# Attention and mixture-of-experts block: three quarters of the tokens' routed experts by sorted group slots instead of all experts for all tokens

## The chip, the core and the metric

One NeuronCore of a Trainium2 chip runs the whole block in one launch. The metric is device time in microseconds (us) of one execution. TensorE does matrix products (PE in the profile, PEld its weight loads), VectorE is DVE, ScalarE is ACT, GpSimd is POOL. SyncE (SP) computes nothing here; it issues transfers (DMAs). Each engine runs its own instructions strictly in order, so an instruction that waits holds up all that stand behind it on that engine.

## The reference, cut to what matters

Two sequences of 1024 tokens of width 128. First causal attention (8 heads, 2 key/value heads through a latent width of 32), with a layernorm before and after and a residual. Then the routed block, here the part that the change touches:

```
scores = sigmoid(x @ gate_weight.T)                    # 32 experts, in 4 groups of 8
sc = scores + gate_bias
group_scores = top_k(sc.reshape(T, 4, 8), 2)[0].sum(-1)
_, gidx = top_k(group_scores, 2)                       # each token keeps 2 of the 4 groups
masked = where(expert in a kept group, sc, -inf)
_, topidx = top_k(masked, 6)                           # 6 experts, all in the kept groups
tw = scores[topidx] / sum * 0.2
routed = sum over the 6: tw * (silu(x @ w_gate[e]) * (x @ w_up[e])) @ w_down[e]
shared = (silu(x @ shared_w_gate) * (x @ shared_w_up)) @ shared_w_down
lg = topidx[:, 0] // 2                                 # one of 16 anchors
anchor = 0.1 * (silu(x @ anchor_w_gate[lg]) * (x @ anchor_w_up[lg])) @ anchor_w_down[lg]
x = x + layernorm(routed + shared + anchor)
```

Expert width is 64, anchor width 32, all numbers are 32-bit floats. The anchor follows from the best expert, so it lies in that expert's group: a token needs only the experts and anchors of its two groups.

## The kernel before, in words

A batch entry is `b` (0 or 1), a tile is 128 tokens, a block is 512 tokens (`BC`), so there are 16 tiles and four blocks.

**Attention** (`attention`, L535 on) goes through 40 steps: a step is one piece of 512 keys for one unit (batch, key/value head, 256 queries). Its order of work is written by hand. Step by step PE gets scores (`numerators`, L464 and L478), the maxima of later units (`maxima`, L399, reduced by DVE at L416), and the weighted values and sums of the step before (L501, L510). Batch 0 goes through its query blocks from first to last, batch 1 from last to first. A block of queries on the diagonal has its exponentials masked by POOL (L487).

**Side work** is a list `side` of generators. Each call of `tick()` advances the generator at the head of the list by one piece and emits its instructions at that place of every engine's order. Attention ticks about twice a step. `route(b)` is such a generator. For all 8 tiles of a batch entry it makes the attention's output projection (L621), the two layernorms, the transposed input `hT` (L313), the logits (L668), then on DVE the choice of groups and experts (`max`, `match_replace`, L692 to L748), and at last the table of weights `cw`: 48 numbers a token (32 experts, 16 anchors). It is transposed and written to DRAM as `cw_rows[b]` (L756).

**Experts** (`experts`, L762 on) does every expert for every token. The 32 experts make 16 chunks of two, the 16 anchors 4 chunks of four; a chunk is 128 hidden units wide. All gate and up weights lie in SBUF (`wg_sb`, `wu_sb`), the down weights too (`wd_sb`). For one block of 512 tokens and each of the 20 chunks (`hidden`, then `down` two chunks later):

- SP issues the spread of the weights from `cw_rows`: rows of DRAM, each broadcast to the 64 or 32 partitions of its expert (L770), into one of 8 buffers;
- PE multiplies `pg` (L775) and `pu` (L776), 512 columns each;
- ACT takes silu (L779), DVE multiplies by `pu` (L780) and by the spread (L781);
- PE adds the chunk to `oacc` with the hidden tile as the moving operand of 512 columns (L785).

The shared expert is one more, first in a block (L791 to L800). `rest()` transposes the 512 results, takes the last layernorm, adds the residual on POOL (L826) and writes them out (L827). The calls stand in the order attention, then blocks (0,0), (0,1), (1,0), (1,1); `route(0)` runs inside attention, `route(1)` inside the first two blocks. PSUM has 7 banks in rotation (`bank`) and one for accumulation (`acc`). PE, DVE, ACT and POOL run in the order in which the program is written; SP's order is left to the scheduler.

Of the kernel before, what the change touches and what calls it, by code (L numbers as in the profile page):

```python
# [17 lines left out]
P = 128  # L18
# [7 lines left out]
def attn_moe_block(  # L26
# [33 lines left out]

    nc = tc.nc
# [20 lines left out]
    NCE = E // EC  # L82
    NCA = A // AC
    NCH = NCE + NCA

# [39 lines left out]
    wg_sb = const.tile([P, NCH, P], F32, name="wg_sb")  # L125
    wu_sb = const.tile([P, NCH, P], F32, name="wu_sb")
    wd_sb = const.tile([P, NCH, D], F32, name="wd_sb")
    for dst, ew, aw in ((wg_sb, w_gate, anchor_w_gate), (wu_sb, w_up, anchor_w_up)):
        nc.sync.dma_start(
            out=dst[:, 0:NCE, :].rearrange("h c (e i) -> h (c e) i", i=MI),  # L130
            in_=ew.rearrange("e h i -> h e i"),
        )
        nc.sync.dma_start(
            out=dst[:, NCE:NCH, :].rearrange("h c (a i) -> h (c a) i", i=AI),
            in_=aw.rearrange("a h i -> h a i"),
        )
    nc.sync.dma_start(
        out=wd_sb[:, 0:NCE, :], in_=w_down.rearrange("(c e) i h -> (e i) c h", e=EC)
    )
    nc.sync.dma_start(  # L140
        out=wd_sb[:, NCE:NCH, :],
        in_=anchor_w_down.rearrange("(c a) i h -> (a i) c h", a=AC),
    )
    swg_sb = const.tile([P, SI], F32, name="swg_sb")
    nc.sync.dma_start(out=swg_sb, in_=shared_w_gate)
    swu_sb = const.tile([P, SI], F32, name="swu_sb")
    nc.sync.dma_start(out=swu_sb, in_=shared_w_up)
    swd_sb = const.tile([SI, D], F32, name="swd_sb")
    nc.sync.dma_start(out=swd_sb, in_=shared_w_down)
# [33 lines left out]
    dram = ctx.enter_context(tc.tile_pool(name="dram", bufs=1, space=bass.MemoryType.DRAM))  # L183
    cw_rows = [dram.tile([E + A, T], F32, name=f"cw_rows{b}") for b in range(B)]
# [3 lines left out]
    ctx.enter_context(tc.manual_schedule(engines={E_.PE, E_.DVE, E_.Activation, E_.Pool}))  # L188
# [136 lines left out]
    def project(b, c):  # L325
# [44 lines left out]
        (b, g, q) for b in range(B) for q in (range(NQ) if b == 0 else reversed(range(NQ)))  # L370
# [164 lines left out]
    def attention(done_with):  # L535
# [39 lines left out]
        for k, (u, s) in enumerate(steps):  # L575
# [11 lines left out]
            tick()  # L587

# [3 lines left out]
            if waiting:  # L592
                last = waiting[0]
                sums(*waiting, o[last])
                if last[0] != u[0]:
                    done_with(last[0])
            waiting = (u, s, pr)
            tick()
            if any(need[j] - done > j - k - 1 for j in range(k + 1, len(steps))):
                one_item()  # L600
                tick()
        weigh(waiting)
        sums(*waiting, o[waiting[0]])
        done_with(waiting[0][0])


    routed = {}

    def route(b):

        while any(u not in ot for u in units if u[0] == b):
            yield
        x1 = x_sb[b]
        norm = Norm(NT, f"attn{b}")
        halves = [range(c * 4, c * 4 + 4) for c in range(NT // 4)]
        an = [work.tile([P, 4, D], F32, tag="xn", name=f"an{b}{c}", bufs=4) for c in range(NT // 4)]
        for c, tiles in enumerate(halves):
            po = bank(f"po{b}{c}")
            for i, t in enumerate(tiles):
                for g in range(G):  # L620
                    nc.tensor.matmul(  # L621
                        po[:, ts(i, P)], lhsT=ot[b, g, t // TQ][:, ts(t % TQ, P)], rhs=ao[:, g, :],
                        start=(g == 0), stop=(g == G - 1),
                    )
            nc.scalar.copy(an[c].rearrange("p t d -> p (t d)"), po)
            yield
        for c, tiles in enumerate(halves):
            norm.stats([an[c][:, i, :] for i in range(4)], 4 * c)
            yield
# [7 lines left out]
        for c, tiles in enumerate(halves):  # L637
# [6 lines left out]
        norm = Norm(NT, f"moe{b}")  # L644
        for c, tiles in enumerate(halves):
# [9 lines left out]
        hT = const.tile([P, T], F32, name=f"hT{b}")  # L655
        hs = []
        for c, tiles in enumerate(halves):
            h = work.tile([P, 4, D], F32, tag="xn", name=f"h{b}{c}", bufs=4)
            for i, t in enumerate(tiles):
                norm.apply_act(h[:, i, :], x1[:, t, :], t)  # L660
            hs.append(h)
            yield
        for c, h in enumerate(hs):
            transposed(h, hT[:, ts(c, BC)], f"h{b}{c}")
            yield
        pl = bank(f"pl{b}")
        for t in range(NT):
            nc.tensor.matmul(pl[:, ts(t, E)], lhsT=hT[:, ts(t, P)], rhs=gwT, start=True, stop=True)  # L668
        score = small.tile([P, NT, E], F32, tag="score", name=f"score{b}", bufs=1)
        loaded[0] = None  # L670
        nc.scalar.activation(score.rearrange("p t e -> p (t e)"), pl[:, 0 : NT * E], AF.Sigmoid)
        yield
        sc = small.tile([P, NT, E], F32, tag="sc", name=f"sc{b}", bufs=1)
        nc.vector.tensor_tensor(
            sc, score, bias_sb.unsqueeze(1).to_broadcast([P, NT, E]), ALU.add
        )
# [3 lines left out]
        g8 = small.tile([P, NT, NG, 8], F32, tag="g8", name=f"g8_{b}", bufs=1)  # L680
        gs = small.tile([P, NT, 16], F32, tag="gs", name=f"gs{b}", bufs=1)
        nc.gpsimd.memset(gs[:, :, NG:8], -BIG)
        nc.gpsimd.memset(gs[:, :, 8:16], BIG)
        ms = small.tile([P, NT, E + 8], F32, tag="ms", name=f"ms{b}", bufs=1)
        nc.gpsimd.memset(ms[:, :, E : E + 8], BIG)
        first = small.tile([P, NT, 8], F32, tag="first", name=f"first{b}", bufs=1)
        nc.gpsimd.memset(first, BIG)

        cw = work.tile([P, NT, E + A], F32, tag="cw", name=f"cw{b}", bufs=1)
        for t in range(NT):  # L690
# [5 lines left out]
        gtop = small.tile([P, NT, 8], F32, tag="gtop", name=f"gtop{b}", bufs=1)  # L696
        for t in range(NT):
            nc.vector.max(gtop[:, t, :], gs[:, t, 0:8])
        nc.vector.memset(gtop[:, :, TOPG:8], BIG)
        yield  # L700
        grep = small.tile([P, NT, 16], F32, tag="grep", name=f"grep{b}", bufs=1)
        for t in range(NT):
            nc.vector.match_replace(grep[:, t, :], gtop[:, t, :], gs[:, t, :], BIG)
        yield

        gm = small.tile([P, NT, NG], F32, tag="gm", name=f"gm{b}", bufs=1)
        nc.vector.tensor_tensor(gm, grep[:, :, 0:NG], gs[:, :, 0:NG], ALU.not_equal)
        nc.vector.tensor_scalar(gm, gm, -0.5, 2.0 * HALF, ALU.add, ALU.mult)
# [3 lines left out]
            gm.unsqueeze(3).to_broadcast([P, NT, NG, EG]),  # L712
# [3 lines left out]
        etop = small.tile([P, NT, 8], F32, tag="etop", name=f"etop{b}", bufs=1)  # L716
        for t in range(NT):
# [3 lines left out]
        yield  # L721
        erep = small.tile([P, NT, E + 8], F32, tag="erep", name=f"erep{b}", bufs=1)
        frep = small.tile([P, NT, E + 8], F32, tag="frep", name=f"frep{b}", bufs=1)
        for t in range(NT):
            nc.vector.match_replace(erep[:, t, :], etop[:, t, :], ms[:, t, :], BIG)
        yield
        for t in range(NT):
            nc.vector.match_replace(frep[:, t, :], first[:, t, :], ms[:, t, :], BIG)
        yield
# [4 lines left out]
        tot = small.tile([P, NT], F32, tag="tot", name=f"tot{b}", bufs=1)  # L734
        nc.vector.tensor_reduce(tot, em, AX.X, ALU.add)
        nc.vector.tensor_scalar(tot, tot, 1e-20, None, ALU.add)
        nc.vector.reciprocal(tot, tot)
        nc.vector.tensor_scalar(tot, tot, 0.2, None, ALU.mult)
# [150 lines left out]
```

## Time and profile before

| what | value |
|---|---|
| device time, median of 3 runs | 480.56 us (479.4 to 482.61) |
| the profiled execution | 480.45 us |
| its span, first to last instruction | 478.7 us |
| TensorE clock granted, mean | 0.984 |
| PE, DVE, ACT, POOL busy | 95%, 63%, 46%, 7% of the span |
| attention ends, first block begins | 233 us |
| block (0,0), (0,1), (1,0), (1,1) from | 233.4, 298.5, 357.4, 412.8 us |
| moved over DMA | 29.26 MB |

The profile of one execution lists for each engine its busy time, then groups of equal instructions by line of the kernel, with count, summed time, mean time of one, and the idle time that stood in front of them with its releaser. The chain that ended last is followed back from the last instruction and says which work set the end. A 32-bit matrix product appears as two MATMUL records, each with its own weight load, so 80 products give 160 records. Matmul records overlap: the distance between their starts, not their duration, is what one costs.

### The profile page before, as it was taken

To read this page: it belongs to the slowest core of one execution; us is meant where nothing else is said; L and a number is where in the kernel's file an instruction comes from. 1 tells how busy PE (TensorE), PEld (TensorE's weight loads), DVE (VectorE), ACT (ScalarE), POOL (GpSimd) and SP (SyncE) were. 2 spreads that over 40 slices of the span, in tenths; PEclk is the share of its full clock that TensorE was granted. 3 is DMA by queue.
4 is the path that set the end of the run, shared out by engine and by line. 5 is a ranking of instruction groups with operands and counts; after the bars stand their busy time and mean duration, and the time that the engine had idled before them with its cause. 6 is when DMAs were issued, how large, how long until landed. Compare 5 with 4: busy or idle time off the path is not lost.

```text
span 478.7 us, 8959 instructions
## 1 busy us (share of the span) xinstructions
PE 453.1 (95%) x3427; PEld 223.7 (47%) x3427; DVE 303.3 (63%) x943; ACT 219.6 (46%) x427; POOL 33.5 (7%) x55
## 2 busy tenths in 40 slices
PE   8997999999999999988869999999999999999991
PEld 5554554544555555555345444544434444344440
DVE  4468766466756887797335575489656755466552
ACT  3454556554554747746642646432225422252222
POOL 2000000000000201002100110000001100001001
PEclk9999999999999999999979999999999999999996
DMA  7820000000000000000521333223151353124100
GB/s 218 222 86 1 2 1 2 1 1 3 1 1 3 2 1 3 1 2 19 176 68 55 100 109 96 66 83 109 51 163 60 118 134 109 66 91 136 58 1 22
DMA packets 27355, 29.26 MB, mean 61 GB/s; under 512 B 8272, under 2 KB 16112, under 8 KB 27312
## 3 DMA queue, kind: packets, MB, share of 16 engines
q1 hardware_dynamic: 26976, 28.15, 19.5%
q8 instruction: 27, 0.44, 0.4%
q10 hardware_dynamic: 336, 0.54, 0.3%
q14 instruction: 16, 0.13, 0.1%
HBM read 27.23 MB, written 1.44 MB: 60 GB/s over the span
## 4 chain that ended last, share of the span: by engine, by line
PE 70%; DVE 16%; issue 10%; ACT 1%; DMA 1%; POOL 0%; POOLq 0%; ACTq 0%; DVEq 0%
PE pg L775 12%; PE pu L776 12%; PE oacc L785 11%; DVE nm L416 8%; PE sm L399 7%; PE s L464 5%; PE o L501 4%; PE o L510 4%; PE pp L352 3%; PE po L621 2%; DVE parts L432 2%; PE psh L791 2%; DVE nm L434 1%; PE s L478 1%; PE sm L409 1%
## 5 line engine op out<-in xcount | busy, mean ns | idle before, releaser
L416 DVE TENSOR_REDUCE nm<-sm 128x1 f32<-128x512 f32 (+2 forms) x192 | 92.7, 548 | 53.1 <-PE sm L409 37.0
L780 DVE TENSOR_TENSOR hid<-hid,pu 128x512 f32<-128x512 f32 x80 | 54.8, 686 | 75.9 <-PE pu L776 56.8
L484 ACT ACTIVATE pr<-s 128x512 f32<-128x512 f32 (+1 forms) x160 | 75.5, 558 | 55.5 <-PE s L478 55.5
L779 ACT ACTIVATE hid<-pg 128x512 f32<-128x512 f32 x80 | 47.8, 597 | 115.5 <-PE pg L775 103.5
L775 PE MATMUL pg<-hT,wg_sb 128*128 128x512 f32 x160 | 83.4, 603 | 0.0
L776 PE MATMUL pu<-hT,wu_sb 128*128 128x512 f32 x160 | 82.1, 594 | 0.0
L785 PE MATMUL oacc<-hid,wd_sb 128*128 128x512 f32 x160 | 80.9, 595 | 0.0
L781 DVE TENSOR_TENSOR hid<-hid,spread 128x512 f32<-128x512 f32 x80 | 58.0, 725 | 2.7
L776 PEld LDWEIGHTS pu<-hT,wu_sb 128*128 128x128 f32 x160 | 30.7, 192 | 38.8 <-issue 37.9
L785 PEld LDWEIGHTS oacc<-hid,wd_sb 128*128 128x128 f32 x160 | 30.1, 190 | 39.3 <-issue 31.5
L464 PE MATMUL s<-qT,kT 32*128 32x256 f32 (+1 forms) x640 | 46.9, 381 | 1.0 <-DVE nm L416 1.0
L775 PEld LDWEIGHTS pg<-hT,wg_sb 128*128 128x128 f32 x160 | 29.3, 192 | 35.7 <-issue 34.8
L399 PE MATMUL sm<-kT,qT 32*128 32x512 f32 (+3 forms) x384 | 44.3, 525 | 0.8 <-DVE nm L416 0.3
L501 PE MATMUL o<-pr,v 128*32 128x256 f32 (+1 forms) x640 | 39.4, 364 | 2.1 <-POOL pr L487 1.9
L464 PEld LDWEIGHTS s<-qT,kT 32*128 32x128 f32 x640 | 32.0, 184 | 16.2 <-issue 10.1
L510 PE MATMUL o<-pr,ones 128*32 128x256 f32 (+1 forms) x640 | 39.3, 363 | 0.0
L487 POOL TENSOR_SCALAR_AFFINE_SELECT pr<-pr 128x1024 f32<-128x1024 f32 x16 | 17.8, 1112 | 196.3 <-ACT pr L484 196.3
L501 PEld LDWEIGHTS o<-pr,v 128*32 128x32 f32 x640 | 16.7, 109 | 23.2 <-issue 10.1
L510 PEld LDWEIGHTS o<-pr,ones 128*32 128x32 f32 x640 | 17.0, 109 | 20.5 <-issue 11.6
L399 PEld LDWEIGHTS sm<-kT,qT 32*128 32x128 f32 x384 | 16.8, 183 | 11.9 <-issue 4.2
L826 POOL TENSOR_TENSOR y<-y,x 128x512 f32<-128x512 f32 x4 | 5.1, 1267 | 192.3 <-DVE y L295 150.7
L478 PE MATMUL s<-mT,ones 32*128 32x512 bf16 (+1 forms) x160 | 16.9, 353 | 1.5 <-DVE mT L447 1.5
(163 smaller groups left out, 365.1 us busy)
## 6 DMA issues: line engine op xcount, KB each, us to landing
spread<-cw_rows SPq DMA_DIRECT2D x128, 128.0 KB, 2.9
spread<-cw_rows SPq DMA_DIRECT2D x64, 64.0 KB, 2.0
out_dram<-y SPq DMA_DIRECT2D x4, 256.0 KB, 2.3
x<-in_L_attn_x_dram SPq DMA_DIRECT2D x2, 256.0 KB, 4.1
wq_sb<-in_L_attn_wq_dram ACTq DMA_DIRECT2D x2, 256.0 KB, 4.2
wo_sb<-in_L_attn_wo_dram SPq DMA_DIRECT2D x1, 512.0 KB, 6.5
x<-in_L_attn_x_dram SPq DMA_DIRECT2D x1, 512.0 KB, 7.6
cw_rows<-cwT SPq DMA_DIRECT2D x4, 96.0 KB, 1.9
```

What stands on the lines that cost most here:

```text
L399: nc.tensor.matmul(banks[r][:, at : at + k1 - k0], lhsT=qT[ts(r, L), g, ts(qt, P)], rhs=kT[ts(r, L), g, k0:k1], start=(at == 0), stop=Fals ...
L416: nc.vector.tensor_reduce(nm[:, k0 // BC, j, r : r + 1], banks[r][:, at : at + k1 - k0], AX.X, ALU.max, negate=True,)
L464: nc.tensor.matmul(banks[r][:, at : at + n], lhsT=kT[rows, g, ts(kt, P)], rhs=qT[rows, g, q * QC + lo : q * QC + lo + n], start=(i == 0), ...
L484: nc.scalar.activation(pr[:, r, 0:m], banks[r][:, 0:m], AF.Exp)
L501: nc.tensor.matmul(o[ts(r, L), lo : lo + n], lhsT=qkv[b][2][:, kt, ts(g, L)], rhs=pr[:, r, at : at + n], start=(kt == 0), stop=False, skip ...
L510: nc.tensor.matmul(o[ts(r, L), QC + lo : QC + lo + n], lhsT=ones32, rhs=pr[:, r, at : at + n], start=False, stop=True, skip_group_check=True,)
L775: nc.tensor.matmul(pg, lhsT=wg_sb[:, c, :], rhs=hT[:, cols], start=True, stop=True)
L776: nc.tensor.matmul(pu, lhsT=wu_sb[:, c, :], rhs=hT[:, cols], start=True, stop=True)
L779: nc.scalar.activation(hid, pg, AF.Silu)
L780: nc.vector.tensor_tensor(hid, hid, pu, ALU.mult)
L781: nc.vector.tensor_tensor(hid, hid, spread, ALU.mult)
L785: nc.tensor.matmul(oacc, lhsT=wd_sb[:, c, :], rhs=hid, start=False, stop=(c == NCH - 1))
```

## The change

Tokens are split. `sparse` is batch 0 and the first half of batch 1 (12 tiles, 1536 tokens); `dense` is the second half of batch 1 (4 tiles, one block). The dense block keeps the 20 chunks of 512 columns, in another order (by group: 4 expert chunks and 1 anchor chunk, five times 128 hidden units a group), with gate and up weights fetched by group. The sparse tokens go another way:

1. At the start the gate and up weights are copied from DRAM to a DRAM tensor `wgu` ordered by group; only the down weights are kept in SBUF. A DRAM tensor `placed` of 15 x 256 rows of 176 numbers is filled with zeros.
2. `route(b, t0, n)` works on parts: (0, tiles 0 to 7), (1, tiles 0 to 3), (1, tiles 4 to 7). For sparse parts it keeps, per token, a row of 128 inputs and 48 weights, and which two groups were chosen.
3. `place()` counts: with triangular and all-ones products on PE, each token's rank in each of its two groups; each group gets whole slots of 256 places (at most 15 slots for 3072 rows). DVE works out each row's place and each slot's group number. POOL then issues 24 indirect DMAs (12 tiles x 2 groups) that scatter 128 rows of 704 bytes each into `placed`, with a small memset ahead of each.
4. `Slots.begin()` loads the group numbers into registers of PE and SP, fetches the rows of the first two slots and transposes them.
5. `Slots.run()` goes through 15 slots: 5 chunks in pairs, gate and up products of 256 columns, silu, two multiplications, and down products with the hidden tile as the stationary operand (128 tokens) and 128 columns of `wd_sb`, picked by the slot's group number. Ahead of that SP fetches the slot's weights (655 KB, by group number), the spread of its weights (six DMAs) and its rows; ACT writes the transposed weights to DRAM and the slot's results to `results`.
6. `gathered(i)`, three times for four tiles each, is side work of the dense block: POOL issues 8 indirect DMAs that gather each token's two result rows, DVE adds both and the shared expert's, and the last layernorm follows.

Attention now goes through batch 1 from first to last query block, with two ticks in batch 1 where there was one. SP's order becomes that of the program too. The list of side work is: the projections, `route(0,0,8)`, `route(1,0,4)`, `place()`, `begin()`, `route(1,4,4)`, and after the slots the three `gathered`.

```diff
+    SL = 256
+    sparse, dense = [(0, 0, NT), (1, 0, NT // 2)], [(1, NT // 2, NT // 2)]
+    NS = TOPG * NTS * P // SL + NG - 1
...
-        (b, g, q) for b in range(B) for q in (range(NQ) if b == 0 else reversed(range(NQ)))
+        (b, g, q) for b in range(B) for q in range(NQ)
...
+        for i, (b, _, t) in enumerate(tiles_of):
+            for k in range(TOPG):
...
+                nc.gpsimd.memset(between, 0.0)
+                move = nc.gpsimd.indirect_dma_start(
+                    out=placed[:, :],
+                    out_offset=bass.IndirectOffsetOnAxis(ap=place_of[:, k, i : i + 1], axis=0),
+                    in_=rows[b][:, t, :], in_offset=None,
+                )
+                tc.declare_no_dep(move.ins, group="placed", reason="no two places are the same")
+                tc.add_to_no_dep_group("placed", move.ins)
+            if i % 2:
+                yield
...
+        def begin(self):
...
+            _, self.numbers = nc.values_load_multi_w_load_instructions(
+                group_no[0:1, 0:16], engines=(E_.PE, E_.SP), min_val=0, max_val=NG - 1,
...
+            self.fetch_rows(0)
+            self.fetch_weights(0)
+            self.fetch_rows(1)
+            yield
+            yield
+            self.turn_rows(0)
+            yield
+            self.fetch_spread(0)
+            self.turn_rows(1)
+            routed["slots"] = True
+            yield
...
+        def turn_rows(self, i):
...
+            pt = bank(f"pt_s{i}")
+            for j in range(JL):
+                nc.tensor.transpose(pt[:, ts(j, P)], self.got[i][:, j, 0:D], ident)
+            for j in range(JL):
+                nc.tensor.transpose(
+                    pt[0 : E + A, SL + j * P : SL + (j + 1) * P], self.got[i][:, j, D : D + E + A], ident
+                )
+            cwT = quarter(f"cwTs{i}")[0 : E + A, :]
+            nc.scalar.copy(cwT, pt[0 : E + A, SL : 2 * SL])
+            nc.scalar.dma_start(out=cw_slots[i], in_=cwT)
+            self.hTp[i] = quarter(f"hTp{i}")
+            nc.scalar.copy(self.hTp[i], pt[:, 0:SL])
...
+        def fetch_spread(self, i):
...
+            own = cw_slots[i][bass.ds(self.numbers[i] * GW, GW), :]
+            half = own[0:EG, :].rearrange("(c e) t -> e c t", e=EC)
+            for e in range(EC):
+                nc.sync.dma_start(
+                    out=t[ts(e, MI), 0:EH, :], in_=half[e].partition_broadcast(MI)
+                )
+            for a in range(AC):
+                nc.sync.dma_start(
+                    out=t[ts(a, AI), EH, :], in_=own[EG + a, :].partition_broadcast(AI)
+                )
...
+        def run(self):
+            while "slots" not in routed:
+                tick()
+            ahead = []
+            for i in range(NS):
+                for k in range(-(-NC // 2)):
+                    ahead.append((i, k, self.hidden(i, k)))
+                    if len(ahead) > 2:
+                        self.down(*ahead.pop(0))
+                    if k == 0:
+                        self.fetch_weights(i + 1)
+                        self.fetch_spread(i + 1)
+                        self.fetch_rows(i + 2)
+                    if k == 1:
+                        self.turn_rows(i + 2)
+                    tick()
...
+    def gathered(i):
...
+        y = [work.tile([P, TB, D], F32, tag="y", name=f"y{name}{k}") for k in range(TOPG)]
+        for t in range(TB):
+            for k in range(TOPG):
+                nc.gpsimd.indirect_dma_start(
+                    out=y[k][:, t, :], out_offset=None, in_=results[:, :],
+                    in_offset=bass.IndirectOffsetOnAxis(
+                        ap=place_of[:, k, i + t : i + t + 1], axis=0
+                    ),
+                )
+        sh = shared(name, slice(t0 * P, (t0 + TB) * P), b)
+        yield
+        py = bank(f"py{name}")
...
+        yield
+        flat = [t.rearrange("p t d -> p (t d)") for t in y]
+        nc.vector.tensor_tensor(flat[0], flat[0], py, ALU.add)
+        nc.vector.tensor_tensor(flat[0], flat[0], flat[1], ALU.add)
+        yield
+        yield from normed(name, b, t0, y[0])
...
+    some = Slots()
+    side += [*(route(*part) for part in sparse), place(), some.begin()]
+    side += [route(*part) for part in dense]
+    attention()
+    some.run()
+    for b, t0, n in dense:
+        while (b, t0) not in routed:
             tick()
+        for c in range(t0 // TB, (t0 + n) // TB):
+            experts(b, c)
```

In the dense block, `tick()` is called twice a chunk. The weights of a slot lie in one of two buffers, the spreads in one of three, the rows in one of three, and the two gathered tiles `y` (two tiles a `gathered`) in the two buffers of that kind.

## The prediction

> **What bounds the kernel now.** I read the page's busy shares first, then the chain, then the costliest groups, and from there the expert stage alone.
>
> ```profile
> PE 453.1 (95%) x3427; PEld 223.7 (47%) x3427; DVE 303.3 (63%) x943; ACT 219.6 (46%) x427; POOL 33.5 (7%) x55
> PE 70%; DVE 16%; issue 10%; ACT 1%; DMA 1%; POOL 0%; POOLq 0%; ACTq 0%; DVEq 0%
> L775 PE MATMUL pg<-hT,wg_sb 128*128 128x512 f32 x160 | 83.4, 603 | 0.0
> L785 PE MATMUL oacc<-hid,wd_sb 128*128 128x512 f32 x160 | 80.9, 595 | 0.0
> L781 DVE TENSOR_TENSOR hid<-hid,spread 128x512 f32<-128x512 f32 x80 | 58.0, 725 | 2.7
> ```
>
> PE is the bound. In the expert stage no DMA is waited for. The chain there, piece by piece (start, length, what):
>
> ```profile
> 140.88 1.98 PE po L621 x16
> 192.10 1.76 PE pl L668 x16
> 357.38 1.86 PE psh L791 x4
> 382.59 0.86 PE pg L775 x2
> 385.16 0.86 PE pg L775 x2
> 412.75 1.86 PE psh L791 x4
> ```
>
> A product of 512 columns costs 0.86 us of PE, a chunk (three) 2.57 us (382.59 to 385.16), an undisturbed block 55.4 us (357.4 to 412.8). The first two rows price small products: 8 of 128 columns take 1.98 us, 0.25 each; 8 of only 32 columns still take 1.76, 0.22 each, so below 128 columns it isn't the columns that set the price (PEld is busy 1.86 of the 1.92 us around those eight: the weight load does).
>
> Transfers: how long SP is held by a spread's issue, and when it lands (the answer for L770 at 226 to 236 us, then for L756); and a POOL instruction over 128 rows.
>
> ```profile
> L770 SPq DMA_DIRECT2D spread<-cw_rows x15: 495/595/1184, 226.0 to 235.5; - x15
> DMA to landing us min/median/max: 2.8/3.1/3.7
> L756 SPq DMA_DIRECT2D cw_rows<-cwT x4: 302/308/325, 224.1 to 345.4; - x4
> DMA to landing us min/median/max: 1.9/1.9/3.2
> L487 POOL TENSOR_SCALAR_AFFINE_SELECT pr<-pr 128x1024 f32<-128x1024 f32 x16 | 17.8, 1112 | 196.3 <-ACT pr L484 196.3
> ```
>
> Last, what an idle PE costs afterwards (stretches; the number after POOL's is the granted clock):
>
> ```profile
> 243.00:245.00 2.00, 0.00 (x0) 0.00 (x0) 0.98 (x2) 0.94 (x2) 0.00 (x0) 1.00 0.38 125
> 247.00:249.00 2.00, 2.00 (x11) 2.00 (x11) 0.00 (x0) 0.00 (x0) 0.00 (x0) 0.50 0.36 119
> ```
>
> About 4 us of idleness were followed by some 7 us at half clock: 3.4 us lost.
>
> **What is removed.** Three of four blocks: 233.4 to 298.5, 298.5 to 357.4, 357.4 to 412.8, so 179.4 us. The fourth, with the tail, is 66.0 us (412.8 to 478.7) and stays.
>
> **Attention, +6.** The half route of batch 1 moves in from the first blocks: 8 output products 1.98, 4 transposes 0.66, 4 logit products 0.96: 3.6 us of PE. `place()` adds 13 narrow bf16 products at about 0.1 (L409: four in 0.40): 1.3. DVE gets some 14 us of routing (half of the 16 tiles' rows of statistics, maxima and replacements) and about 4 us for `place()`; DVE is busy 65.9 of 88 us in batch 1, so between 0 and 18 us of it shows; I take 3, since PE is at 82 of 88. The end gains: three short diagonal steps that wait for POOL's mask become one, -2. Attention would end at 239 us, if nothing in it waited.
>
> **The scatter, +32.** Counting the pieces of side work against the ticks: the 24 scatters are emitted from step 36 (of 0 to 39), and `turn_rows(0)`, which needs all of them landed, stands in PE's order just ahead of step 38. The cover is two steps. Maxima are finished by then, and such a step takes 3.0 us (scores 1.08, products against ones 0.25, values 0.85, sums 0.85). The last step to the first product after it took 5.9 us in the profile (227.4 to 233.3), so step 38 begins at 239 - 5.9 - 3.0 = 230 and step 36 at 224. POOL: 24 x (indirect DMA + memset 0.12). The trace has no indirect DMA. Below, 0.30, the shortest issue on SP; above, 2.4, if each waited for a landing. I take 1.1, what POOL itself needs for an instruction over 128 rows (L487), because it is POOL that has to issue these, each with a list of 128 places. 24 x 1.22 = 29.3: 224.5 to 253.8. Landing 1.9: 255.7. `fetch_rows(0)` on SP, which stands behind that wait with the weights of slot 0 behind it: 2.3 to land (as the 256 KB output does): 258. PE stands still for 28 us, with ACT, DVE and steps 38 and 39 behind it. With transposes 0.7 and the half clock 3.4: 32. The slots begin at 271. Loading the group numbers into PE's registers falls into the same wait; it costs nothing unless that wait is gone, then at most some us.
>
> The Trainium skill, "DMA: Bandwidth & Descriptors", section "Anatomy of one DMA", gives a DMA issued from GpSimd about 2.0 us plus its bytes at 436 GB/s, most of it completion; no run here shows that yet. By the page, 90 KB take 2.2 us each, and if scatters did not overlap their sum would be 53 us and not 29; the nearest row here, 1.9 us for SP's 96 KB, is a landing and not an issue.
>
> **The slots, +136.** PE per slot: 10 products of 256 columns at 0.43 (half of 0.86; not below 0.25) 4.3; 10 of 128 columns at 0.24, 2.4; four transposes about 0.5: 7.2 us. DVE 2 x 1.4 + 0.8 = 3.6, ACT about 3.5: hidden. But there is a ring: turning slot i+1's rows lets ACT write its weights; SP's spread of i+1 waits for that write; the rows of slot i+2 stand behind that spread on SP; and PE turns them in its own order, four chunks later. Its length: transposes 0.7, ACT copy 0.45, issue and landing 1.9 plus 0.1; six spread issues (2 x 0.6, 4 x 0.4) 2.8 and their register arithmetic 0.6 (0 to 2, not in the trace); rows to landing 2.3 to 2.8: about 9.2 us. It is longer than 7.2, so it sets the pace: 12 turns x 9.2 = 110, the first 3.7, the last two slots and the rest 18. `route(1,4,4)` runs there and costs ACT its table loads (1.28 us each): +4. Sum 136. Data: 1.5 MB a slot, 160 GB/s at this pace; the trace held 240 to 260 in most of the first 28 us, so bandwidth is no bound unless small rows halve it.
>
> **The gathers, +31.** The dense block keeps 55.4. In it, DVE's add of `gathered(0)` stands behind chunk 1, about 7 us in. The results land 2.9 us after the last product, 8 gathers x 1.1 = 8.8, landing 2: 13.7 us in. PE runs on as long as banks last (7): it loses about 4.5. The next `gathered` needs both `y` buffers: free only when the output has landed, 7.5 us after the statistics begin (470.2 to 477.7 in the tail shown by the trace), plus one chunk of DVE 1.4, gathers 8.8, landing 2, adds 1.4: 21 to 21.5 us from add to add. In that time DVE's order lets PE have three chunks, 7.7. So 13.8 lost, twice. With 4.5 that is 32, less 0.9 for the merged shared product. Everything of it hangs on DVE's order; the spreads queued behind the output DMA on SP are two buffers ahead.
>
> **Start and others, 0.** The reordering copies and the zero fill queue on SP behind the inputs, in the first 40 us, and are wanted after 220. The outer time is 480.45 - 478.7 = 1.75; the profiled run is 0.1 below the median.
>
> **Sum:** 478.7 - 179.4 + 6 + 32 + 136 + 31 = 504.3; with 1.75: 506 us.
>
> **Rivals.**
> - *The indirect DMAs are cheap* (ends faster). For it: the issue time needn't grow with the pieces; SP issued the 1024 pieces of `wo` in 0.39 us and the 64 rows of a spread in 0.60. Each 0.1 us less is worth 2.4 in the scatter and about 2.2 in the gathers. At 0.30: 506 - 0.8 x 46 = 469. It decides from 0.53 us down, where the time equals that of before. Against: the issue is not SP's.
> - *The ring fits into PE's 7.2 us*: 12 x 2.0 less, 482. For it: landings here go down to 1.8. Against: seven issues stand in a row in it.
> - *Transfers crowd*: rows of 1 KB, and a write of weights that shares the engines with 655 KB. At 11.5 us a slot 12 x 2.3 more, 534.
> - *Indirect DMAs follow one another with their landings*: 2.4 us each, 1.2 us more for 48, most of it exposed, 560. Against: scatters are declared independent.
>
> **How the numbers follow.** Mine 0.48 (490 to 522), cheap 0.18, ring hidden 0.14, crowding 0.12, serial 0.08. Predicted: 506. The range 466 to 536 leaves out the serial case, the low end of the cheap one and the high end of crowding. Less than 1% (4.8 us) can't be told from no change. Faster: cheap 0.16, ring 0.05, mine 0.01: 0.22. Same: 0.02 + 0.06 + 0.03 = 0.11. Slower: 0.44 + 0.03 + 0.12 + 0.08 = 0.67.
>
> **What would show it.** PE idle for some 28 us ahead of the first turned rows, released by a DMA, with POOL busy all that time and the clock at half after it; slots 9 us apart with PE waiting for rows; two stops of DVE of over 10 us in the dense block, released by gathers. The prediction is wrong if POOL's issues are under 0.6 us, if turned rows never wait, or if gathers land before their adds.

## The result, and the profile after

The changed kernel takes 543.4 us (median of 4 runs, 540.9 to 547.0) where the kernel before took 480.7 beside it (4 runs, 479.4 to 482.6): 1.131 times the time, 95% interval 1.123 to 1.138. Forecast were 506, with 466 to 536. The direction came out, and so did the stop at the scatter and the ring of the slots; the move was 62.7 us, where the forecast, from the 480.6 known then, was 25.4. The profiled run took 543.64 us and spans 541.9.

First the page's header, busy shares, slices of the span and chain, of the kernel after:

```profile
span 541.9 us, 10069 instructions
PE 429.9 (79%) x3726; PEld 266.8 (49%) x3726; DVE 285.3 (53%) x969; ACT 221.6 (41%) x455; POOL 84.1 (16%) x155
...
PE   8989999999989888973047687888678886649991
...
POOL 3000000000121002008820010000000014535000
PEclk9999999999999898777559897998989998587997
...
PE 36%; DVE 19%; DMA 15%; POOL 9%; issue 8%; ACT 5%; SPq 5%; POOLq 0%; DVEq 0%; ACTq 0%
```

TensorE was 95% busy and 70% of the chain; now it is 79% and 36%. It lost only 23 us of work (453.1 to 429.9) for three blocks removed, since the 15 slots bring theirs back in smaller products. DMA and POOL, once 1% of the chain together, hold 24%. In the slices PE falls to 3 and 0 while POOL shows 8 and 8: that is the scatter. The 6s and the 4 near the end, again beside POOL, are the gathers. The granted clock is low there, and already in the end of attention, ahead of the scatter (the first two 7s). TensorE was at half clock for 108 us of the trace, against 17 before.

The stop before the slots, on PE's timeline (start, length, engine, line, what, and in brackets the idle time before it and what ended it):

```profile
247.43 1.07 PE L547 MATMUL o<-pr,ones 128*32 128x256 f32 x16 [0.37 <-issue]
278.64 0.69 PE L961 MATMUL pt_s<-ident,got 128*128 128x128 f32 x2 [30.15 <-DMA got<-placed]
...
289.35 0.83 PE L547 MATMUL o<-pr,ones 128*32 128x256 f32 x16
290.11 1.13 PE L1000 MATMUL pgs<-hTp,wbs 128*128 128x256 f32 x4
```

Forecast were 28 us; it is 30.15. Attention's last steps (until 290.2) come behind the stop. POOL in the same stretch, its first three scatters:

```profile
244.34 1.17 POOL L898 DMA_INDIRECT placed<-rows,place_of  x1 [2.81 <-DVE place_of L892]
245.52 0.11 POOL L897 MEMSET between<- 128x1 f32 x1
245.81 0.96 POOL L898 DMA_INDIRECT placed<-rows,place_of  x1 [0.18 <-issue]
246.78 0.11 POOL L897 MEMSET between<- 128x1 f32 x1
247.08 1.03 POOL L898 DMA_INDIRECT placed<-rows,place_of  x1 [0.19 <-issue]
```

An indirect DMA holds POOL for 0.96 us, and with memset and gaps the 24 follow each other at 1.28 (244.3 to 273.7); I had put 1.22. But the first starts at 244.3 and not at 224.5.

What waited, in total, times, longest (answer on waits, kernel after):

```profile
PE pt_s L961 <- DMA got<-placed: 57.4, 14, 30.1
...
PE pyg L1099 <- DVE shg L1063: 18.0, 3, 9.7
...
DVE yg L1105 <- DMA yg<-results,place_of: 14.4, 3, 5.8
...
PE rank L844 <- DVE mb L837: 3.9, 1, 3.9
...
POOL yg L1089 <- DMA out_dram<-yg: 3.8, 2, 2.0
```

The first line is the ring: beside the 30.1 of the scatter, PE waited 27 us for rows at 13 other slots, which went by every 10.2 us (turned rows at 320.3 and, ten slots later, at 422.4). The second is where TensorE itself stops beside the gathers: the shared expert's product for a gathered group waits for VectorE's multiplication, which in the two long ones stands in VectorE's order behind the add and norm of the group before. The third is VectorE's wait for the gathers. The fourth belongs to `place()`, inside attention. The last is the wait that I had blamed for the stops at the gathers, and it is small.

| stretch | forecast | measured | off by |
|---|---|---|---|
| first scatter | 224.5 | 244.3 | +19.8 |
| first product of a slot | 271 | 290.1 | +19.1 |
| slots | 136 | 149.0 (to 439.1) | +13.0 |
| dense block, gathers, tail | 97.3 | 102.8 (to 541.9) | +5.5 |

The last three add up to the 37.6 by which the span was missed.

### The profile page after: what moved, and what is told of

Read it like the earlier page. It is cut to its first block, busy times and chain, and to the rows that moved or that the text cites. A ratio compares the mean times of both kernels' runs of the same rounds, so it can differ in the third digit from the quotient of the medians.

```text
span 541.9 us, 10069 instructions
## 1 busy us (share of the span) xinstructions
PE 429.9 (79%) x3726; PEld 266.8 (49%) x3726; DVE 285.3 (53%) x969; ACT 221.6 (41%) x455; POOL 84.1 (16%) x155
## 4 chain that ended last, share of the span: by engine, by line
PE 36%; DVE 19%; DMA 15%; POOL 9%; issue 8%; ACT 5%; SPq 5%; POOLq 0%; DVEq 0%; ACTq 0%
DVE nm L453 7%; DMA got<-placed 7%; PE sm L436 5%; PE s L501 4%; POOL placed L898 4%; POOL yg L1089 4%; PE o L538 4%; PE o L547 3%; SPq L983 3%; DMA wbs<-wgu 3%; PE pp L389 2%; PE pa L1000 2%; SPq L979 2%; DMA cw_slot<-cwTs 2%; PE oacc L1159 2%
## 5 line engine op out<-in xcount | busy, mean ns | idle before, releaser
L1008 DVE TENSOR_TENSOR hids<-hids,pus 128x512 f32<-128x512 f32 x30 | 20.6, 686 | 71.0 <-ACT hids L1007 47.4
L501 PE MATMUL s<-qT,kT 32*128 32x256 f32 (+1 forms) x640 | 53.3, 402 | 5.8 <-DVE nm L453 5.2
L961 PE MATMUL pt_s<-ident,got 128*128 128x128 f32 x30 | 7.5, 338 | 57.4 <-DMA got<-placed 57.4
L1089 POOL DMA_INDIRECT yg<-results,place_of x24 | 24.3, 1011 | 129.8 <-issue 125.7
L1023 PEld LDWEIGHTS ys<-wd_sb,hids 128*128 128x128 f32 x300 | 41.7, 197 | 2.7
L1023 PE MATMUL ys<-wd_sb,hids 128*128 x300 | 41.4, 279 | 0.0
L1007 ACT ACTIVATE hids<-pgs 128x512 f32<-128x512 f32 x30 | 17.9, 596 | 37.5 <-PE pgs L1000 37.4
L1000 PE MATMUL pgs<-hTp,wbs 128*128 128x256 f32 x120 | 31.8, 389 | 0.0
L1000 PE MATMUL pus<-hTp,wbs 128*128 128x256 f32 x120 | 30.8, 379 | 0.0
L1149 ACT ACTIVATE hid<-pg 128x512 f32<-128x512 f32 x20 | 11.8, 597 | 44.5 <-PE pg L1145 44.5
```

The lines of the kernel that those rows point to most:

```text
L501: nc.tensor.matmul(banks[r][:, at : at + n], lhsT=kT[rows, g, ts(kt, P)], rhs=qT[rows, g, q * QC + lo : q * QC + lo + n], start=(i == 0), ...
L1000: nc.tensor.matmul(p[:, lo : lo + SL], lhsT=wb[:, m, ts(c, P)], rhs=hT, start=(lo == 0), stop=(c == pair[-1]), skip_group_check=True,)
L1007: nc.scalar.activation(hid[:, 0:n], pg[:, 0:n], AF.Silu)
L1008: nc.vector.tensor_tensor(hid[:, 0:n], hid[:, 0:n], up, ALU.mult)
L1023: nc.tensor.matmul(o[:, ts(j, D)], lhsT=hid[:, at : at + P], rhs=w, start=(c == 0 and j == 0), stop=(c == NC - 1), skip_group_check=True,)
L1089: nc.gpsimd.indirect_dma_start(out=y[k][:, t, :], out_offset=None, in_=results[:, :], in_offset=bass.IndirectOffsetOnAxis(ap=place_of[:, k ...
```

## The experiments

Each is one profiled run against the kernel before on the same chip (477.8 to 480.9), unless an interval is given. The kernel after varied by 6 us from run to run, so single runs are read by their stages, and differences of 3 us are not read at all.

### Where attention's 24 us come from

**a1_ascending and a5_ascending_timed**: the kernel before with one edit.

```diff
-for q in (range(NQ) if b == 0 else reversed(range(NQ)))
+for q in range(NQ)
```

> The kernel before with one edit: attention goes through batch 1 from first to last query block. Theory (attention got long because routing and counting fill VectorE in batch 1): the order alone costs little, the first expert block begins at 230 to 237 us (233.4 before), total 478 to 486. Rival (the order itself, with the long steps last): the first block begins at 243 us or later, total 490 or more.

> The kernel before with the second batch of the attention taken from first to last, as in the earlier run of the same edit (471.8 us), now with an interval: 470 to 474, about 1.5% under the kernel before. If that run was a lucky one: 476 to 482.

471.8, then 472.99 (4 runs), ratio 0.985, interval 0.982 to 0.988. The first expert block begins at 231.4 (before: 233.3), as expected:

```profile
231.40 1.07 PE L791 MATMUL psh<-hT,swg_sb 128*64 128x512 f32 x2
```

The rest of the gain, which I had not expected, comes behind it, so the total fell below the forecast 478. The kernel before, then this one, by stretches (PE, PEld, DVE, ACT, POOL busy, then granted clock and DMA):

```profile
243.00:250.00 7.00, 3.42 (x15) 3.42 (x16) 2.47 (x5) 0.96 (x3) 0.00 (x0) 0.67 0.25 76
```

```profile
243.00:250.00 7.00, 7.00 (x27) 3.86 (x26) 3.88 (x13) 1.78 (x3) 0.00 (x0) 1.00 0.21 76
```

The stop in the first block, with its half clock, is gone. So the order is no cost: alone it gains 1.5%, and this one-line edit is the fastest kernel of the study. Why the stop goes with the order was not tested, and the kernel after has no expert block at that place, so nothing shows that it keeps this part of the gain.

**a2_ascending_two_ticks**: the same, and two ticks for one in batch 1 (`if u[0]: tick()` twice a step).

> The kernel before with the ascending order and two ticks in batch 1, so that routing of batch 0 is packed into the first half of batch 1's steps, as in the changed kernel; routing of batch 1 stays under the expert blocks. Theory: packing costs up to 6 us (first block at 234 to 241), and the rest of the 18 to 20 us is the half route of batch 1 and the counting. Rival (the packing is all of it): first block at 250 us or later.

482.8; the first block begins at 242.4:

```profile
242.38 1.07 PE L795 MATMUL psh<-hT,swg_sb 128*64 128x512 f32 x2
```

Packing the side work costs 11.0 us, not up to 6. Part of it is the clock: from 185 to 220 it was granted at 0.85 here, 5 us of full clock lost, and at 1.00 in a1.

**a4_one_tick**: the kernel after without the doubled ticks (the two `if u[0]: tick()` removed).

> The kernel after without the doubled ticks of the attention's second batch. The question is which of two terms makes up the 24 us by which the scatters of the kernel after came later than the first expert block of the kernel before. Theory (the route of the second batch's first half and the places are one chain of small VectorE instructions; the scatters can start only at its end, packed or not): the attention ends about 11 us earlier, and the chain that is then left runs with TensorE stopped; the scatters begin at 240 to 248 as in the kernel after (244.3), and the time is within 5 us of 543. Rival (the packing itself costs the 11 us that it cost in the kernel before): the scatters begin at 231 to 237 and the time is 530 to 536.

553.5, and both theories missed: the scatters begin at 259.9, later than in the kernel after. Its PE timeline:

```profile
234.65 0.83 PE L547 MATMUL o<-pr,ones 128*32 128x256 f32 x16
242.54 1.63 PE L350 MATMUL pt_h<-ident,rows 128*128 128x128 f32 x4 [7.05 <-ACT rows L342]
244.85 1.92 PE L715 MATMUL pl<-upT,hT 128*128 128x32 f32 x8 [0.68 <-ACT hT L351]
256.21 0.22 PE L840 MATMUL rank<-mb,before 128*128 128x48 bf16 x1 [9.45 <-DVE mb L833]
```

Attention is over at 235.5, 4 us behind a1. Then route and places run alone, a chain of short instructions with PE stopped for most of the time, and the first scatter starts 24 us later. So doubled ticks lose 11 us inside attention to save more behind it.

**a6_begin_behind**: the slots' beginning, with the first turned rows, moved behind attention's last step.

```diff
-side += [*(route(*part) for part in sparse), place(), some.begin()]
-side += [route(*part) for part in dense]
+side += [*(route(*part) for part in sparse), place()]
 attention()
+side += [some.begin(), *(route(*part) for part in dense)]
```

> The kernel after, with the beginning of the slots (rows 0 and 1, weights, the first turned rows) written behind the attention's last step instead of among its side work. In the kernel after, TensorE's stop of 30.15 us stands ahead of the last steps of the attention, which end at 290.2. Theory (these steps depend on nothing that is scattered and run while POOL scatters): they end at about 258, the turned rows still come at about 279, the slots begin 8 to 10 us earlier: 533 to 536. Rival (the scatters come later by as much, or the route of the last four tiles takes the gain): within 3 us of 543.

538.6, half of the forecast gain, and not more than the kernel after varies from run to run. By stages, the slots begin at 281.3 for 290.1, the 8 to 10 us forecast, but end only 2.4 us earlier (436.7 for 439.1). All steps but the last ran on (their last product starts at 252.2), and then PE stopped again, for another reason. The waits of this kernel between 240 and 290 us:

```profile
PE o L538 <- POOL pr L524: 21.4, 1, 21.4
PE pt_s L961 <- DMA got<-placed: 2.4, 1, 2.4
```

The last step's causal mask is a POOL instruction, and it stood behind the 24 scatters. One wait took the place of the other. Why the slots then lost most of their lead was not tested.

### What the stop at the scatter is

**s1_half_scatter**: the kernel after, `for k in range(1)` for `range(TOPG)` at the scatters.

> The kernel after, with only the first choice of each token scattered: 12 of the 24 scatters and of their memsets. The other choice's places stay zero, so its rows are left out of the computation; the number of slots, their loads and matmuls stay as they are. Theory (the stop of TensorE before the first turned rows is the POOL's own string of scatters, 1.265 us from one to the next in the kernel after): 12 x 1.265 = 15.2 us less, the wait of pt_s falls from 30.15 to about 15, the span by 15 to 18 (half clock after a shorter stop included), time 525 to 529. Rival (the stop is the landing of the writes, or something else that is late, such as the route of the last four tiles): the wait stays above 25 us and the time above 537.

526.1, and the longest wait for the turned rows is halved (waits of this kernel, 230 to 300 us):

```profile
PE pt_s L961 <- DMA got<-placed: 18.3, 3, 15.0
```

30.1 to 15.0 for 12 scatters less: 1.26 each. The stop is POOL's string of issues. The last scatter starts at 273.7 and the rows that wait for it are issued at 276.2, so only 2.5 us are end and landing. The Trainium skill, "DMA: Bandwidth & Descriptors", section "Anatomy of one DMA", calls descriptor generation small and most of its 2.0 us completion. Here landings overlapped, and what added up was POOL's 0.96 us of issue with the memset and the gaps; the measurement decides.

### What the rows of the ring stand behind

Five kernels change only SP's work of a slot. The original order is: weights of slot i+1 (640 KB), its spread (two transfers of 256 KB, four of 32), rows of slot i+2 (176 KB).

**r1_rows_first**: rows ahead of both. **r5_rows_second**: rows between them.

```diff
+self.fetch_rows(i + 2)        # r1
 self.fetch_weights(i + 1)
+self.fetch_rows(i + 2)        # r5
 self.fetch_spread(i + 1)
-self.fetch_rows(i + 2)
```

> The changed kernel with the rows of slot i+2 issued on SP ahead of weights and spread of slot i+1. Theory (a ring through ACT's write, the spread and the rows sets the slots' pace of 10.2 us): PE no longer waits for rows; pace 7.3 to 8.5 us, total 20 to 36 us shorter (508 to 524). Rival (transfers crowd, or PE is the bound): pace over 9.7 us, total within 6 us of 543.

> The kernel after with the rows of slot i+2 issued between the weights and the spread of slot i+1, so behind the weights' 640 KB but ahead of the spread's wait for its written weights and of its 640 KB. The runs with fewer bytes and fewer issues gave 0.7 to 0.95 us a slot of the 2.45 that all rows first gave. Theory (the spread is what the rows stand behind: 2.8 us until its weights are written, then 5.6 and more of issues and transfer; the weights cost little): the period falls to 7.6 to 8.2, time 512 to 522. Rival (the weights' bytes and the wait for their buffer matter as much): the period stays above 9, time 528 or more.

513.6 and 513.7; a slot every 7.75 us in both (r1: ten from 313.7 to 391.2). Rows behind the spread are the whole loss; the weights ahead of them cost nothing that can be measured, though the rows then take 4.5 us to land instead of 2.4: they are issued early enough.

**r2_three_spreads**: one transfer of 128 KB for the four of 32.

```diff
-for a in range(AC):
-    nc.sync.dma_start(out=t[ts(a, AI), EH, :], in_=own[EG + a, :].partition_broadcast(AI))
+nc.sync.dma_start(out=t[:, EH, :], in_=own[EG, :].partition_broadcast(P))
```

> The kernel after with the four small spreads of a slot (32 KB each, one per anchor row) replaced by one of 128 KB that spreads the first anchor's row over all 128 partitions: the same bytes in three issues for six. The other three anchors' weights are left out of the computation. The rows of slot i+2 stay behind them on SP. Theory (the ring's period was sized too small because each issue holds SP's queue: four small spreads took 2.97 us from the first to the end of the fourth ahead of the rows): three issues fewer are about 2.2 us less ahead of the rows, the period falls from 10.2 to about 8.0 to 8.5, over the 14 further slots 24 to 30 us: 513 to 522. Rival (the bytes in flight and the landing times set the period, not the number of issues): 538 to 546.

542.3: no change, and the theory fell. SP's queue in one slot of the kernel after, then of this one:

```profile
353.14 0.36 SPq L912 DMA_DIRECT2D wbs<-wgu  x1
354.37 1.46 SPq L979 DMA_DIRECT2D spreads<-cw_slot  x2
356.03 2.00 SPq L983 DMA_DIRECT2D spreads<-cw_slot  x4
358.07 0.42 SPq L951 DMA_DIRECT2D got<-placed  x1
```

```profile
351.17 0.33 SPq L912 DMA_DIRECT2D wbs<-wgu  x1
352.39 1.42 SPq L979 DMA_DIRECT2D spreads<-cw_slot  x2
354.03 0.44 SPq L982 DMA_DIRECT2D spreads<-cw_slot  x1
354.51 0.43 SPq L951 DMA_DIRECT2D got<-placed  x1
```

The rows are issued 2.1 us behind the first spread instead of 3.7, but PE turned them at 360.0, 7.6 us behind it, where the kernel after needed 6.5 (360.9). In the answer on DMAs their median landing went from 3.1 in the kernel after,

```profile
got<-placed SPq DMA_DIRECT2D x15, 176.0 KB, 3.1
```

to 4.7 here:

```profile
got<-placed SPq DMA_DIRECT2D x15, 176.0 KB, 4.7
```

The reading that fits is that what SP issued earlier waited in the transfers' queue for the bytes ahead of it. With the rows first (r1) the same line reads:

```profile
got<-placed SPq DMA_DIRECT2D x15, 176.0 KB, 2.4
```

The Trainium skill, same page, section "Queues, rings and completion order", has each DMA engine take the descriptors of a ring in order; the landing of the rows, 2.4 us when they go first and 4.7 behind weights and spread, agrees.

**r3_small_weights** and **r4_small_weights_three_spreads**: from slot 2 on only 64 of the weights' 640 KB are fetched, in the same place and behind the same wait; r4 has r2's three spreads too.

```diff
+if 2 <= i < NS:
+    wb = self.wbs[i] = self.wbs[i - 2]
...
+    nc.sync.dma_start(out=wb[:, 0, (NC-1)*P : NC*P], in_=src[:, 0, (NC-1)*P : NC*P])
```

> The kernel after, with a tenth of the weights' bytes from the third slot on: the weights' transfer of a slot stays in its place on SP and waits for the same matmul, but brings only the last 64 KB of the 640; the other nine tenths are those of the slot two before, so most slots compute with another group's weights. All six spread issues stay. Theory (two limits lie side by side from the weights' issue to the rows' landing, 7.7 to 8.3 us in the kernel after: the issues on SP, 4.9 us before the rows are issued and 2.4 to 2.8 of landing, and the 1.3 MB that must move ahead of the rows; so taking one away leaves the other): the rows land about 2.4 us behind their issue and the period falls by 0.3 to 0.6 us: 533 to 540. Rival (the bytes alone set the ring): the period falls to TensorE's own 7.3 to 7.9, time 505 to 520.

> The run with small weights and the run with three spread issues together (a tenth of the weights' bytes, one spread of the first anchor's row in place of four). Theory of two limits side by side: with both gone the rows are issued 3.4 us behind the weights and land 2.4 to 2.8 later, 5.9 to 6.2 for 7.7 to 8.3; with 1.6 us from the turned rows to the next weights' issue the ring takes 7.6 to 7.8, about TensorE's own pace, and 14 slots gain 2.1 to 2.6 each: 506 to 514. Rival (something else in the ring, such as the landing of the group weights or the wait for the weights' buffer, sets the period): 530 or more.

532.7 and 529.0: periods of 9.5 and 9.25 for 10.2. r3 came just under what two limits side by side would give; r4 missed it by 15 us. In r4 the rows are issued 2.1 to 2.5 us behind the first spread and turned 5.6 to 6.6 behind it: the spread's own 640 KB are left ahead of them, and in most slots 3.1 to 3.4 us pass from turned rows before the next spread starts at all.

### The gathers

**g1_six_tiles**: six `y` buffers for two (`bufs=6`).

> The changed kernel with six buffers for the gathered tiles in place of two, so that all 24 gathers can be issued as soon as the results have landed. Theory (each further group of gathers waits for the output of the one before it): from add to add 10 us in place of 21, 15 to 25 us shorter (518 to 528). Rival (POOL's issue of 24 gathers is itself the wait): within 6 us of 543.

542.9: no change. My reason fell; the first two adds were still 19.4 us apart (459.7 and 479.2; in the kernel after 20.5).

**g2_gathers_up_front**: all 24 gathers issued ahead of the first add, six buffers. **g3_adds_late**: and 20 empty yields ahead of the first add.

```diff
+for i in range(0, NTS, TB):
+    gather(i)                      # the 8 indirect DMAs of gathered(i)
...
+side.append(iter([None] * 20))     # g3 only
 for i in range(0, NTS, TB):
     side.append(gathered(i))       # without its DMAs
```

> The kernel after, with all 24 gathers issued one behind the other ahead of the first add, into six y buffers. Theory (the second and third group of gathers come late because they are written on POOL behind the residual add of the group before, not because a buffer is missing): the 24 gathers take 24 x 1.26 = 30 us in one string, the adds come about 10 us apart instead of 19.4, the second and third wait of the add for its gathers nearly vanish, and the dense block gains most of what it lost between 460 and 490 us: time 528 to 537. Rival (DVE's own work in the adds and norms sets the distance): adds still over 17 us apart and the time 540 to 545.

> The kernel before this one in the list with 20 empty yields ahead of the first add, so that the adds are written behind the tenth chunk of the dense block, when the gathers should have landed. Theory: no add waits for a gather, VectorE never stops in front of the dense block's products, and TensorE gets back the 16.6 us it lost in 450 to 490 us together with the half clock behind them: time 520 to 529. Rival (the adds late push the last norms behind the block): the stop moves to the end, and the time stays within 3 us of the run with all gathers up front.

534.4 and 532.9. From first gather to end the kernel after needs 97.2 us (444.7 to 541.9), g2 87.2, g3 82.3; in total g3 shows less, because its first gather came 4 us later in that run (448.7). The wait of the adds is one of 5.8 us in g2, where it was three of 14.4 in sum:

```profile
DVE yg L1114 <- DMA yg<-results,place_of: 5.8, 1, 5.8
```

and in g3 there is none. So the order on POOL caused the second and the third wait of the adds: a group's eight gathers are written behind the residual add of the group before (L1076), which waits for VectorE's norm. It is not all of the loss. TensorE's own wait beside the gathers, 18.0 us in the kernel after, stayed in g2:

```profile
PE pyg L1108 <- DVE shg L1065: 15.2, 3, 9.1
```

The longest of these, 9.1, still has the first add's 5.8 us in it; the last, 4.7 us, comes with no wait for gathers: the adds and norms in VectorE's order, ahead of the multiplication that TensorE needs, hold it up by themselves. So the adds of g2 came 14.9 and 17.1 us apart, not 10. In g3 TensorE's wait is 7.1, and 4.9 us more are gained behind the first gather, though by its total g3 stayed with the rival. Even so g3 needs 88.4 us from the slots' end to its own end, 22 more than the 66.0 of the kernel before; what the rest is was not separated.

### Together, and another shape

**c2_rows_first_adds_late** is r1 with g3; **c3_all_repairs** adds a6.

> The kernel after with both repairs: the rows of slot i+2 issued ahead of the weights and the spread of slot i+1, all gathers up front and the adds late. Theory (the two costs lie in different stretches and add): 513.6 less what the late adds gain, 15 to 22 us: 491 to 499. Rival (one hides the other): 503 or more.

> The kernel after with three repairs: rows first, all gathers up front with the adds late, and the slots' beginning behind the attention. Theory (three stretches that add): 495.9 less 8 to 10: 485 to 489. Rival (one hides the other): 492 to 497.

495.9 and 496.0. The two repairs add, 47.5 us together; r1 and g3 by their totals were 29.8 and 10.5, and 14.9 is what g3 gained behind its first gather. a6 brings nothing on top: the slots begin 7.6 us earlier and end 1 us earlier (405.9 for 407.1). The traces show part of the difference: in c3's slots TensorE waits 7.7 us for weights and 1.7 for rows, in c2's 0.4 and none.

**v1_eight_tiles**: only the first four tiles of each batch go through places (`sparse = [(0, 0, TB), (1, 0, TB)]`, 11 slots), single ticks, a dense block between attention and slots to cover places and scatters, r1 and g3 in it.

> A version that keeps the slots where they pay: only eight tiles (the first four of each batch) go through places, 11 slots for 15; the second half of batch 0 goes through a dense block right behind the attention, and the routes, the places and the 16 scatters run beside it; rows are issued ahead of weights and spreads, all gathers are issued in one string, and the adds are written late in the last dense block. Theory (each stop found can be hidden behind a dense block): attention as with the ascending order alone, 231; a dense block 60; 11 slots at 7.9 = 87; start and end of the slots 5 to 12; a dense block with the tail 62: 445 to 457 us, against 471.8 of the kernel before with the ascending order. Rival (the stops come back in other places: VectorE too full in the first dense block, the first slot waits for its rows and its spread): 460 to 475.

499.6 (4 runs), 1.041 times the time before, interval 1.039 to 1.044: 43 us above the forecast range, and 25 above the rival's. The scatters, meant to run early in the block that begins at 235.9, came at its end:

```profile
L894 POOL DMA_INDIRECT placed<-rows,place_of x16: 959/963/1173, 288.8 to 308.0; - x16
```

Routes and places had to share VectorE with the block (17.6 of 20 us busy from 240 to 260), which itself took longer: 77 us to the first turned rows (312.9) where I had 60. The slots took 108 for 92 with their start, the last block 77 for 62. These 48 us, and 5 by which the first block began late, are the miss against the 445. Why the slots ran at 9.8 us on average was not tried; in the trace the last four are 7.0 us apart, and TensorE waits twice for rows between the slots, 2.6 and 5.7 us.

## Why the prediction was wrong, by its steps

- **Three blocks removed, 179.4**: right; it is not in doubt in any run.
- **Attention, +6: the step that failed most.** Without the stop, attention would end near 256 (a6: the last step but one ends at 253.2, and a step takes 2.5 to 3), not 239: about +22. Of that, measured against a1 (231.4): 11 are the doubled ticks (a2), 4 the work that moves in with single ticks (a4), and about 9, if these two add, are left for the second batch's half route and `place()`, of which 3.9 is PE's wait for `mb` in the middle. A part of the whole is a cost that the step did not have at all, the half clock: from 210 to 244 the kernel after was granted 0.75, 8.5 us of full clock lost, where a1 had 1.00 from 200 to 231. How much of that delayed the end is not separated. I had counted PE's 3.6 us and let 3 of VectorE's 18 show. The bound I wrote down, "between 0 and 18", was the honest one; I took a value from its low end because PE was at 82 of 88 us, though maxima and routing alternate on one VectorE, which was busy for 9.45 of the 10 us from 225 to 235. That VectorE's order is the reason is read from the traces; no run took the routing off it. The 2 us for the steps at the end were right (a1: 1.9).
- **The scatter, +32**: right in mechanism, and s1 shows it: 30.15 for 28, POOL's 0.96 for 1.1, the half clock behind it (until 282.0). The price was luck in part: I took it from a mask of 1024 columns, which shares nothing but the engine and the 128 rows with an indirect DMA. That cover was short was right too; that the mask of the last step also stands behind the scatters on POOL was missed (a6), and would have ended the cover anyway.
- **The slots, +136**: the ring is real (r1, r5: -30 us by order alone) and PE's own pace of 7.2 was near (7.75 without the ring). Its size failed: 9.2 forecast, 10.2 measured. The start of the spread, put at 3.15 us behind the turned rows, was near (2.8 in most slots); the piece from there to the next turned rows was put at 3.4 of issue and 2.3 to 2.8 of landing, and took 6.5 to 7.7. I priced the rows as if they moved alone, and they land behind weights and spread (r2, r3, r4). How much of the excess is issue and how much bytes does not separate cleanly: taking either away, or both, left most of it.
- **The gathers, +31**: size near (the stretch was 5.5 longer), by luck, since the reason was wrong. Not the buffers (g1; 3.8 us of wait) but POOL's program order (g2) and the adds and norms in VectorE's order (g3), and some 22 us stay unexplained. The sign I had named, two stops of VectorE of over 10 us, did not come: there were three, the longest 5.8.
- **Rivals**: *cheap indirect DMAs* are excluded by 0.96 us on POOL, *serial landings* by the 1.28 us spacing. *Ring hidden* is excluded; *crowding* came nearest, with 1.0 of its 2.3 us a slot (10.2, not 11.5). The point from which cheap DMAs would have decided is 0.55 us by the prices given there, not 0.53.

The measured time lay above the range because I held attention's term fixed: its upper bound, 15 us more (18 of VectorE's work for 3), was left out of it and would have reached 551.

## What to carry to other kernels

When side work is packed into an engine's order to be early, price it on the engine that is serial in it (here VectorE's small instructions), against that engine's gaps, not against the busy time of the engine that bounds the kernel. For each transfer that a ring waits for, list what stands ahead of it twice: the instructions on the issuing queue and the bytes already given to the transfers; moving the small and urgent one to the front gave here 30 us for one line. And before explaining a late transfer by a missing buffer, look at what is written ahead of it on the engine that issues it.

## What was not expected of the hardware

- An indirect DMA of 128 rows costs POOL the same whether it scatters rows of 704 B (0.960 us) or gathers rows of 512 B (0.944): the price does not go by the bytes, and 48 of them are some 46 us of one engine. The medians, from the answers on the two tiles:

```profile
L898 POOL DMA_INDIRECT placed<-rows,place_of x24: 956/960/1172, 244.3 to 273.7; - x24
L1089 POOL DMA_INDIRECT yg<-results,place_of x24: 940/944/1422, 444.7 to 495.9; - x24
```

- Half the issues with the same bytes was worth nothing (r2), a tenth of the weights' bytes with the same issues 0.7 us a slot (r3).
